# Zeroing and filling arrays of diagonals in DRAM, in large transfers or in parts, in a state-space scan kernel

## The chip, the cores and the metric

The kernel runs on one core of a Trainium2 chip. The metric is the device time of one execution in microseconds. The median of three runs before the change is 3376.29 us (3375.55 to 3376.74).

## The reference, cut to what matters

Two layers work on an image batch x of shape (4, 32, 32, 256). The second (linear attention, then a mixture of 16 experts) is not touched by the change. The first normalises x, multiplies it up to 512 channels, applies a 3 x 3 depthwise convolution and gelu, and runs a selective state-space scan over the 1024 positions of each image, with 64 states for each of the 512 channels:

```python
        proj = x @ w_x
        dt_raw, Bm, Cm = jnp.split(proj, [R, R + N], axis=-1)      # R = 16, N = 64
        dt = jax.nn.softplus(dt_raw @ w_dt + dt_bias)
        A = -jnp.exp(A_log)

        def step(h, inp):
            xt, dtt, Bt, Ct = inp
            dA = jnp.exp(dtt[:, :, None] * A)
            h = dA * h + (dtt * xt)[:, :, None] * Bt[:, None, :]
            y = jnp.einsum('bdn,bn->bd', h, Ct)
            return (h, y)
```

The change concerns Bt alone, and how it gets to one of the places where it is multiplied by dtt * xt.

## The kernel before

**Units, states and slots.** The scan is cut into 8 units: 4 images by 2 halves of 512 positions (`units`, L256; `u` or `w` is a unit's number, and odd units are second halves). In a unit, 64 states are gone through in turn, and in a state the 512 channels in four blocks of 128 (`m`). One state and one block is a slot; a unit has 64 x 4 = 256 slots, numbered `k` over everything and `at` within the unit.

**What a slot does.** ScalarE computes the decay, exp(dt A), for four slots ahead (`decay`, L925). The product dt x B of a state is made, for each of four groups of 128 positions (`j`), from `dtxT`, which lies with positions on the partitions: ScalarE scales it by B (`scale`, L903) into `bx`, and TensorE transposes it into a PSUM bank, three slots ahead (`turn`, L931). For the first group there are three ways, given for every state by a letter in `KINDS`: A is ScalarE; P is GpSimd (POOL, `scale_apart`, L913, tile `bxp`); D is TensorE alone, by multiplying `dtxT` with a diagonal matrix that carries B's 128 entries (L935). VectorE then runs the recurrence over 512 positions as one scan instruction (`scan`, L954). It writes into a ring of four states (`ring`, `RING = 4`). Behind a state's fourth block, GpSimd multiplies the state by C's row (L961), and in the first half of an image a small transfer saves the state's last column for the second half (L966, `last<-h`, 128 x 4 numbers). TensorE adds the states up by transposes that accumulate in PSUM, 11 slots behind (`add_up`, L968).

**The diagonals.** D needs, for each state n, a 128 x 128 matrix with B on its diagonal and zeros elsewhere. These matrices lie in DRAM, in two arrays of 64 matrices each, `diag_b[0]` and `diag_b[1]` (L247); unit w uses array w % 2. A tile of zeros is copied over each array once (`zero_diagonals`, L251: 4 MB each, rows of 512 B), at slots 4 and 14 (L1122). For every unit but the first, one transfer writes B's entries onto the 64 diagonals: 64 x 128 elements, 4 bytes each, with a step of 129 elements (L505, in `put_bc`). It follows the copy of B and C out of PSUM into the tile `bct` (L500) and the transfer of C into DRAM (L502, `cd<-bct`). `fetch_diagonal` (L897) loads a state's matrix, 64 KB, three states ahead, into one of three buffers.

**The SyncE queue.** All of these transfers are issued on SyncE's queue (SP), in program order, and an instruction that waits there holds all that follow. In a state SP issues C's row for three states on, spread over the partitions (`fetch`, L877, 256 KB, tile `cb_n`, four buffers), a diagonal matrix where the letter is D, and in first halves `last`; besides them loads of x, of the convolution's tap matrices (`dgc<-diags`, L402), of residual rows, and, in unit 6, the next layer's weights (L738 to L746).

**The order.** The order in each engine's stream is fixed when the program is built: the loop over slots (L1108) emits the slot's work, and then takes pieces of the other work (the next units' normalisation, convolution, projection and dt; the last unit's output) from lists made by `beside` (L995). A piece is (gap in slots from the one before, engine, cost, function, whether it takes or frees the spare PSUM bank, a thing it needs done). Each part of a list is spread evenly over a stretch of slots given in `EVEN`, `ODD` or `START`; of all lists whose next piece is due, the earliest is taken, within a budget for each engine and slot (`MOST`; SP's cost is 0). B and C of unit u + 1 are made in unit u by `dt_bc`'s first part (`dt0`); `dt1` begins at slot 50 in even units, 61 in odd ones and 52 in unit 0.

Of the kernel before, what the change touches and what calls it, by code (L numbers as in the profile page):

```python
# [16 lines left out]
P = 128  # L17
# [5 lines left out]
def over_middle(ap, n):  # L23

    return ap.unsqueeze(1).to_broadcast([ap.shape[0], n, ap.shape[1]])
# [8 lines left out]
def conv_ssm_attn_moe_kernel(ctx: ExitStack, tc: tile.TileContext, a: dict, out: bass.AP):  # L34
    nc = tc.nc
# [6 lines left out]
    NS = a["L0_conv_A_log"].shape[1]  # L42
# [4 lines left out]
    DK = DN // P  # L47
# [83 lines left out]
    def blk(i, n=BANK):  # L131
        return slice(i * n, (i + 1) * n)
# [12 lines left out]
    with ExitStack() as l0:  # L145
# [20 lines left out]
        with nc.allow_non_contiguous_dma(reason="small, once"):  # L166
            for m in range(DK):
                nc.scalar.dma_start(
                    out=cw[:, m, :],
                    in_=a["L0_conv_conv_w"][:, :, 0, m * P : (m + 1) * P].rearrange(  # L170
                        "i j p -> p (i j)"
                    ),
# [7 lines left out]
            out=w_dt[R : R + 1, :], in_=a["L0_conv_dt_bias"].rearrange("(o d) -> o d", o=1)  # L180
# [66 lines left out]
        diag_b = [dram.tile([NS, P, P], F32, name=f"diag_b{k}") for k in range(2)]  # L247
        zero = scanp.tile([P, P], F32, name="zero", tag="dgb", bufs=3)
        nc.vector.memset(zero, 0.0)

        def zero_diagonals(k):  # L251
            nc.sync.dma_start(
                out=diag_b[k].rearrange("n a b -> a n b"), in_=over_middle(zero, NS)
            )

        units = [(b, seg) for b in range(NB) for seg in range(NHALF)]  # L256
        made = {}
        done = set()
# [14 lines left out]
        def piece(gap, eng, cost, what, bank="", need=None):  # L273
            return gap, eng, cost, what, bank, need
# [6 lines left out]
        def logs(rs, mv):  # L281
            nc.scalar.activation(rs, mv, AF.Ln, bias=eps5)
# [172 lines left out]
        def dt_bc(w, needs):  # L455
# [42 lines left out]
            def put_bc():  # L498
                t = pre.tile([P, BANK], F32, name="bct")
                (nc.scalar.copy if on_scalar("bc") else nc.vector.tensor_copy)(t, made["bg"])  # L500
                cd = dram0.tile([NS, BANK], F32, name="cd")
                nc.sync.dma_start(out=cd, in_=t[NS:, :])  # L502
                if w > 0:
                    with nc.allow_non_contiguous_dma(reason="diagonals"):
                        nc.sync.dma_start(  # L505
                            out=diag_b[w % 2].rearrange("n a b -> n (a b)")[:, :: P + 1],
                            in_=t[:NS, :P],
                        )
                made["cd", w] = cd

            for j in range(TPB):
                for m in range(0, DK, 2):
# [117 lines left out]
            for m in range(DK):  # L630
# [3 lines left out]
                    lambda m=m: (put_dtx(m), done.add(("dt", w)) if m == DK - 1 else None), "free",  # L634
                ))
            return parts + [todo]

        def after_stats(u):
            made["mv"] = pre.tile([P, TPB, 2], F32, name="mv")
# [201 lines left out]
        def on_scalar(what):  # L841

            return not alone and what in APART[made["u"] % 2]
# [15 lines left out]
        at = [i for i, p in enumerate(conv_1) if p[4] == "free"][2] + 1  # L859
# [135 lines left out]
        def beside(u):  # L995


            n = len(units)
            v = u + 2
            made["u"] = u  # L1000
            at = START if u == 0 else ODD if u % 2 else EVEN
            dts = [at[f"dt{i}"] for i in range(5)]
            lists = [[([
                piece(1, "PE", 0.22, lambda m=m, j=j: skip(u, m, j))
                for m in range(DK) for j in range(TPB)
            ], at["skip"])]]
            if v < n:
                b, half = units[v]
                if u == 0:
                    lists.append([  # L1010
                        (head(b, 0), at["head"]), (head(b, 1), at["head1"]), (conv(v), at["conv"]),
                    ])
                elif half == 0:
                    lists.append([(head(b, 1), at["head"]), (conv(v), at["conv"])])
                else:
                    lists.append([(conv(v), at["conv"])])
                    if b + 1 < NB:
                        lists[-1].append((head(b + 1, 0), at["head"]))
            if v == n:
                lists.append([(matrices(), MATS)])  # L1020
            if u > 0:
                lists.append([(after_stats(u - 1), at["stats"])])
            if u + 1 < n:
                lists.append(list(zip(dt_bc(u + 1, ("st", u - 1) if u > 0 else None), dts)))
            else:
                lists.append([([
                    piece(1, "ACT", 1.5, lambda: logs(made["rs"], made["mv"][:, :, 1]),
                          need=("st", u - 1)),
                    piece(1, "ACT", 0.2, lambda: roots_after(u - 1)),
                ], dts[2])])  # L1030
            if u > 0:
                lists.append(list(zip(after(u - 1, ("rs", u - 1)), (at["after0"], at["after1"]))))
            return [
                [(lo + (hi - lo) * i / len(part), *p)
                 for part, (lo, hi) in l for i, p in enumerate(part)]
                for l in lists
            ]
# [55 lines left out]
        with tc.manual_schedule():  # L1093
            alone = False
            nc.scalar.preload_act_table_set("natural_log_exp_and_others")
            n_all = len(steps) * DK
            for s in range(4):
                fetch(s)
            for k in range(8):
                scale(*divmod(k, DK))  # L1100
            for s in range(4):
                scale_apart(s)
            for k in range(4):
                decay(*divmod(k, DK))
            for k in range(3):
                turn(*divmod(k, DK))
            lists, free, free_at, holds = [], True, 0, None
            for k in range(n_all + LAG):  # L1108
                u, at = divmod(k, SLOTS)
                if k + 8 < n_all:  # L1110
                    scale(*divmod(k + 8, DK))
                if k + 4 < n_all:
                    decay(*divmod(k + 4, DK))
                if k < n_all:
                    scan(*divmod(k, DK))
                    if k % DK == DK - 1 and k // DK + 4 < len(steps):
                        scale_apart(k // DK + 4)
                if k >= LAG:
                    add_up(*divmod(k - LAG, DK))
                if k + 3 < n_all:  # L1120
                    turn(*divmod(k + 3, DK))
                if k in (4, 14):  # L1122
                    zero_diagonals(1 if k == 4 else 0)
                if at % DK == 1 and k > DK and k // DK + 3 < len(steps):
                    fetch(k // DK + 3)
                    if by_diagonal(k // DK + 3, 0):
                        fetch_diagonal(k // DK + 3)
                if k >= LAG and at == LAG - 1 and u > 0:
                    close_sum(u - 1)
                if u == len(units):  # L1130
                    continue
                if at == FIRST:
                    lists = beside(u)
                    ready = [k] * len(lists)
                if at < FIRST:
                    continue
                used = dict.fromkeys(("PE", "DVE", "ACT", "POOL", "SP", ""), 0.0)
                while True:
                    best = None
                    for i, l in enumerate(lists):  # L1140
                        if not l or ready[i] + l[0][1] > k or l[0][0] > at and i != holds:
                            continue
                        when, _, eng, c, _, pb, need = l[0]
                        if need and need not in done:
                            continue
                        if pb == "take" and not (free and free_at < k):
                            continue
                        if used[eng] > 0 and used[eng] + c > MOST.get(eng, 9.0):
                            continue
                        if best is None or when < best[0]:  # L1150
                            best = when, i
                    if best is None:
                        break
                    i = best[1]
                    _, _, eng, c, what, pb, _ = lists[i].pop(0)
                    what()
                    ready[i] = k
                    used[eng] += c
                    if pb == "take":
                        free, holds = False, i  # L1160
                    elif pb == "free":
                        free, free_at, holds = True, k, None
                assert at < SLOTS - 1 or not any(lists), [len(l) for l in lists]
# [628 lines left out]
    for o in range(NB):  # L1792
        n = o + 1 if o + 1 < NB else None
# [407 lines left out]
    for e in (*range(SOON, NE), *range(SOON)):  # L2201
        todo += [k for k in fixed if k[1] == e]
        n = len({k[1] for k in todo if k not in soon})
# [46 lines left out]
```

## Time and profile before

| what | us |
|---|---|
| median of three runs | 3376.29 |
| profiled execution, its own time | 3389.96 |
| span of the profiled execution | 3387.8 |
| scan, first to last VectorE scan instruction (L954) | about 130 to 2690 |
| VectorE scans (L954), 2048 of 1.2 us and 1.26 us mean | 2387.7 busy |
| whole transfer of B's entries (L505), 7 of them, issue to landing | 15.9 median |
| `last<-h` (L966), 256 of them, issue to landing | 3.1 median |
| C's row (L880), 512 of them, issue to landing | 3.3 median |
| diagonal matrix (L900), 100 of them, issue to landing | 3.2 median |

The profile records one execution with start and end of every instruction. Busy time of an engine is the sum of its instructions; before each instruction the profile gives the engine's idle time and what ended it (the releaser). DMA transfers appear twice: as an instruction on the queue that issues them (SP), where a long duration means that the issue itself was held, and as a time from issue to landing. PE is the matrix engine and PEld its weight loads; DVE is VectorE, ACT is ScalarE, POOL is GpSimd. PEclk is the granted clock of TensorE, 1.00 being full.

### The profile page before, as it was taken

To read this page: it belongs to the slowest core of one execution; us is meant where nothing else is said; L and a number is where in the kernel's file an instruction comes from. 1 tells how busy PE (TensorE), PEld (TensorE's weight loads), DVE (VectorE), ACT (ScalarE), POOL (GpSimd) and SP (SyncE) were. 2 spreads that over 40 slices of the span, in tenths; PEclk is the share of its full clock that TensorE was granted. 3 is DMA by queue.
4 is the path that set the end of the run, shared out by engine and by line. 5 is a ranking of instruction groups with operands and counts; after the bars stand their busy time and mean duration, and the time that the engine had idled before them with its cause. 6 is when DMAs were issued, how large, how long until landed. Compare 5 with 4: busy or idle time off the path is not lost. (4 is left out here: it accounts for less than half of the span.)

```text
span 3387.8 us, 62750 instructions
## 1 busy us (share of the span) xinstructions
PE 3172.2 (94%) x23407; PEld 2753.3 (81%) x23407; DVE 2886.9 (85%) x3435; ACT 2717.3 (80%) x4621; POOL 2718.4 (80%) x1215
## 2 busy tenths in 40 slices
PE   7899999999999999999999999989999889789998
PEld 4588888988898888888988988768778756589998
DVE  4699999999999999999999999999999867652222
ACT  1699999999999999999999999899999754322221
POOL 0488998999999989999998999899999842234443
PEclk9999999999999999999999999999999999999999
DMA  3552224224333332253334223423222210467785
GB/s 105 150 68 63 68 66 69 71 71 62 67 78 69 68 72 76 62 63 74 73 73 68 71 64 60 71 54 68 60 62 67 80 48 29 156 186 231 214 245 149
DMA packets 423835, 300.76 MB, mean 89 GB/s; under 512 B 225073, under 2 KB 329393, under 8 KB 423522
## 3 DMA queue, kind: packets, MB, share of 16 engines
q1 hardware_dynamic: 397202, 274.25, 32.9%
q0 software_dynamic: 14016, 18.05, 2.8%
q10 hardware_dynamic: 12304, 4.37, 0.5%
q8 instruction: 187, 3.06, 0.4%
q14 instruction: 126, 1.03, 0.1%
HBM read 262.34 MB, written 34.87 MB: 88 GB/s over the span
## 5 line engine op out<-in xcount | busy, mean ns | idle before, releaser
L961 POOL TENSOR_TENSOR h<-h,cb_n 128x2048 f32<-128x2048 f32 x512 | 2154.9, 4226 | 142.6 <-DVE h L954 89.9
L928 ACT ACTIVATE da<-dt,l_conv_a_log_sb 128x512 f32<-128x512 f32 x2048 | 1438.3, 714 | 32.4 <-DVE h L954 31.3
L908 ACT ACTIVATE bx<-dtxT,proj 128x512 f32<-128x512 f32 x1748 | 1246.9, 714 | 29.9 <-DVE dtxT L600 16.4
L975 PE MATMUL y<-ident,h 128*128 128x128 f32 x8192 | 1236.5, 274 | 8.9 <-POOL h L961 5.8
L954 DVE TENSOR_TENSOR_SCAN h<-da,last,ps 128x512 f32<-128x512 f32 x1024 | 1217.9, 1262 | 7.0 <-PE ps L940 1.8
L954 DVE TENSOR_TENSOR_SCAN h<-da,ps 128x512 f32<-128x512 f32 x1024 | 1169.8, 1201 | 41.8 <-DMA last<-h 16.8
L940 PE MATMUL ps<-ident,bx 128*128 128x128 f32 x6992 | 1119.0, 276 | 41.7 <-DVE h L954 29.4
L975 PEld LDWEIGHTS y<-ident,h 128*128 128x128 f32 x8192 | 979.0, 141 | 99.9 <-issue 20.6
L940 PEld LDWEIGHTS ps<-ident,bx 128*128 128x128 f32 x6992 | 819.7, 142 | 101.8 <-DVE h L954 81.1
L2015 DVE TENSOR_TENSOR hT<-s,p 128x256 f32<-128x256 f32 x146 | 61.4, 421 | 281.0 <-ACT s L2014 281.0
L940 PE MATMUL ps<-ident,bxp 128*128 128x128 f32 x800 | 237.6, 297 | 58.9 <-DVE h L954 46.0
L2033 POOL DMA_INDIRECT out_dram<-yb,src x73 | 116.0, 1589 | 212.3 <-DVE yb L2030 82.2
L2014 ACT ACTIVATE s<-p 128x256 f32<-128x256 f32 x146 | 56.1, 384 | 265.4 <-PE p L2008 262.6
L413 PE MATMUL bg<-pad,dgc 128*128 128x256 f32 x864 | 258.2, 380 | 0.4 <-DMA dgc<-diags 0.4
L940 PEld LDWEIGHTS ps<-ident,bxp 128*128 128x128 f32 x800 | 112.3, 140 | 142.0 <-DVE h L954 89.2
L919 POOL TENSOR_SCALAR bxp<-dtxT,proj 128x512 f32<-128x512 f32 x200 | 147.0, 735 | 59.5 <-DVE dtxT L600 59.5
L935 PE MATMUL ps<-dgb,dtxT 128*128 128x128 f32 x800 | 170.3, 295 | 22.5 <-DMA dgb<-diag_b 9.7
L2008 PE MATMUL p<-xT,w 128*128 128x128 f32 x1408 | 171.7, 275 | 2.2 <-ACT xT L1988 2.2
L2008 PEld LDWEIGHTS p<-xT,w 128*128 128x128 f32 x1408 | 167.4, 192 | 5.0 <-ACT xT L1988 2.9
L935 PEld LDWEIGHTS ps<-dgb,dtxT 128*128 128x128 f32 x800 | 120.5, 190 | 49.2 <-DVE h L954 36.2
L413 PEld LDWEIGHTS bg<-pad,dgc 128*128 128x128 f32 x864 | 130.5, 191 | 0.7 <-DMA dgc<-diags 0.7
L2008 PE MATMUL p<-xT,m 128*128 128x128 f32 x928 | 115.4, 278 | 0.0
(341 smaller groups left out, 2681.6 us busy)
## 6 DMA issues: line engine op xcount, KB each, us to landing
cb_n<-cd SPq DMA_DIRECT2D x512, 256.0 KB, 3.3
m<-in_L_ffn_w_dram SPq DMA_DIRECT2D x87, 512.0 KB, 5.6
w<-in_L_ffn_w_dram SPq DMA_DIRECT2D x60, 512.0 KB, 6.9
dgc<-diags SPq DMA_DIRECT2D x84, 192.0 KB, 3.1
diag_b<-zero SPq DMA_DIRECT2D x2, 4096.0 KB
dgb<-diag_b SPq DMA_DIRECT2D x100, 64.0 KB, 3.2
last<-h SPq DMA_DIRECT2D x256, 2.0 KB, 3.1
xd<-xe SPq DMA_DIRECT2D x8, 512.0 KB, 3.5
```

The lines of the kernel that those rows point to most:

```text
L413: nc.tensor.matmul(made["bg"].rearrange("p (h w) -> p h w", w=WW)[:, blk(c, deep), :], made["dgc", m * 3 + i][:, j, :], pads[m][:, at : at ...
L908: nc.scalar.activation(t, made["dtxT", u][:, j, :], AF.Copy, scale=made["proj", u][:, j, R + n : R + n + 1])
L919: nc.gpsimd.tensor_scalar(t, made["dtxT", u][:, 0, :], made["proj", u][:, 0, R + n : R + n + 1], 1.0, ALU.mult, ALU.mult,)
L928: nc.scalar.activation(t, made["dt", u][:, m, :], AF.Exp, scale=A[:, m, n : n + 1])
L935: nc.tensor.matmul(t[:, blk(j, P)], made["dtxT", steps[s][0]][:, j, blk(m, P)], made["dgb", s], start=True, stop=True,)
L940: nc.tensor.transpose(t[:, blk(j, P)], made["bx", s, j][:, blk(m, P)], ident)
L954: nc.vector.tensor_tensor_scan(h[:, m, 1:], made.pop(("da", s, m)), made.pop(("dbx", s, m)), 0.0 if seg == 0 else last[b][:, n, m : m + 1] ...
L961: nc.gpsimd.tensor_tensor(h[:, :, :BANK], h[:, :, 1:], over_middle(made["c", s], DK), ALU.mult)
L975: nc.tensor.matmul(made["y", u][j][:, blk(m, P)], made["h", s][:, m, blk(j, P)], ident, is_transpose=True, start=n == 0 and m == 0, stop=n ...
L2008: nc.tensor.matmul(p12[:, j, s, :], w_of(w, key)[:, ck, blk(h + j, P)], on_b["xT", key][:, ck, :], start=(ck == 0), stop=(ck == CK - 1),)
L2015: nc.vector.tensor_tensor(on_b["hT", key][:, h : h + 2, :], s, p12[:, :, 1, :], ALU.mult)
L2033: s = nc.gpsimd.indirect_dma_start(of[:, :], bass.IndirectOffsetOnAxis(src[:, c : c + 1], 0), yb, None, bounds_check=NB * L - 1, oob_is_er ...
```

## The change

The 4 MB transfers of zeros are cut into eight parts each, of 8 states (1024 rows of 512 B). They are issued at the third slot of each of the first 16 states, array 1 first. The transfer of B's entries is cut into eight parts too, of 8 states x 128 elements. They are taken out of `put_bc` and become pieces of a list of their own on SP, at least 4 slots apart, spread over 40 slots from the first slot of `dt1` on; they need the copy into `bct`. Transfers that write and read the arrays keep their content.

```diff
-        def zero_diagonals(k):
+        part_of = NS // 8
+
+        def zero_part(i):
+            k, n = 1 - i // 8, (i % 8) * part_of
             nc.sync.dma_start(
-                out=diag_b[k].rearrange("n a b -> a n b"), in_=over_middle(zero, NS)
+                out=diag_b[k][n : n + part_of].rearrange("n a b -> a n b"),
+                in_=over_middle(zero, part_of),
             )
...
                 cd = dram0.tile([NS, BANK], F32, name="cd")
                 nc.sync.dma_start(out=cd, in_=t[NS:, :])
-                if w > 0:
-                    with nc.allow_non_contiguous_dma(reason="diagonals"):
-                        nc.sync.dma_start(
-                            out=diag_b[w % 2].rearrange("n a b -> n (a b)")[:, :: P + 1],
-                            in_=t[:NS, :P],
-                        )
+                made["bct", w] = t
                 made["cd", w] = cd
+                done.add(("bct", w))
...
+        def entries(w):
+
+            def part(i):
+                with nc.allow_non_contiguous_dma(reason="diagonals"):
+                    nc.sync.dma_start(
+                        out=diag_b[w % 2].rearrange("n a b -> n (a b)")[
+                            blk(i, part_of), :: P + 1
+                        ],
+                        in_=made["bct", w][blk(i, part_of), :P],
+                    )
+
+            return [piece(4, "SP", 0, lambda i=i: part(i), need=("bct", w)) for i in range(8)]
...
                 lists.append(list(zip(dt_bc(u + 1, ("st", u - 1) if u > 0 else None), dts)))
+                lists.append([(entries(u + 1), (at["dt1"][0], at["dt1"][0] + 40))])
...
-                if k in (4, 14):
-                    zero_diagonals(1 if k == 4 else 0)
+                if k % DK == 2 and k // DK < 16:
+                    zero_part(k // DK)
```

## The prediction

> **What bounds the kernel now.** I read, in order: busy time by stretches, who waited for whom at the scan line, SyncE's instructions around the two kinds of transfer that the change cuts up, and VectorE's instructions at the same moments.
>
> The stretches first (columns: stretch, its length, then busy us of PE, PEld, DVE, ACT, POOL with counts, granted TensorE clock, DMA share, GB/s).
>
> ```profile
> 1000.00:1300.00 300.00, 292.18 (x2304) 264.22 (x2303) 296.60 (x272) 290.81 (x467) 282.96 (x102) 1.00 0.33 71
> 1300.00:1600.00 300.00, 285.06 (x2255) 256.89 (x2254) 294.14 (x276) 292.69 (x475) 289.13 (x112) 0.99 0.35 68
> ```
>
> From about 130 to 2690 us VectorE works 98 to 99% of the time. It is the bound of the state scan, with the others a few per cent behind; the span follows what keeps VectorE idle. SyncE (SP) only issues transfers, so its work costs nothing until something on VectorE's path waits for it. What the scan's VectorE instructions waited for (us, times):
>
> ```profile
>   DMA last<-h: 16.8, 5
>   PE ps L940: 10.3, 40
>   ACT da L928: 8.9, 18
> ```
>
> The largest item is five waits for the small transfer that saves a state's last column (L966). It reads the slot of the ring of four that VectorE wants to overwrite four states later. SyncE at those moments (start, us on SP, queue, line, operation):
>
> ```profile
> 135.25 0.62 SPq L252 DMA_DIRECT2D diag_b<-zero  x1
> 138.80 10.24 SPq L880 DMA_DIRECT2D cb_n<-cd  x1
> ...
> 152.99 0.69 SPq L252 DMA_DIRECT2D diag_b<-zero  x1
> 153.78 14.46 SPq L966 DMA_DIRECT2D last<-h  x1
> ...
> 195.38 0.60 SPq L505 DMA_DIRECT2D diag_b<-bct  x1
> 196.07 9.96 SPq L966 DMA_DIRECT2D last<-h  x1
> ```
>
> Ordinarily an L966 issue takes 0.6 us and an L880 issue 0.32. Straight behind a transfer of 8192 rows (zeros: 128 x 64 rows of 512 B; B's entries: 64 x 128 elements of 4 B) the next issue is held for 10 to 14 us, and SP issues in order. VectorE then (in brackets its idle time before, and the releaser):
>
> ```profile
> 170.82 4.55 DVE L954 TENSOR_TENSOR_SCAN h<-da,ps 128x512 f32<-128x512 f32 x4 [5.83 <-DMA last<-h]
> 211.57 3.44 DVE L954 TENSOR_TENSOR_SCAN h<-da,ps 128x512 f32<-128x512 f32 x3 [2.81 <-DMA last<-h]
> 846.16 4.55 DVE L954 TENSOR_TENSOR_SCAN h<-da,ps 128x512 f32<-128x512 f32 x4 [2.35 <-DMA last<-h]
> 2126.25 5.67 DVE L954 TENSOR_TENSOR_SCAN h<-da,ps 128x512 f32<-128x512 f32 x5 [3.01 <-DMA last<-h]
> 2134.37 0.69 DVE L552 TENSOR_SCALAR dt<-bg 128x512 f32<-128x512 f32 x1 [2.46 <-PE bg L541]
> ```
>
> The fifth wait is at 1487.00, 2.82 us. So of seven transfers of entries only those in units 0, 2, 4 and 6 stall VectorE; units 1, 3 and 5 are second halves of a batch and save no column. There the held instruction is a load of C's row (L880), and only POOL waits, 0.92 to 1.51 us, which VectorE doesn't feel.
>
> **What goes: the zeros.** The two transfers of 4 MB become 16 of 512 KB (1024 rows each). The 5.83 us go, and 0.52 us just after. Before it, ScalarE sat 4.78 us for a load of x stuck in the same queue; VectorE felt 0.87 + 0.28 us of that. Together 7.5 us. Not all can return: from 142 to 168 us PE is nearly without a gap (projections and skip products besides the scan's own), and VectorE already lost 2.02 us to it at 154. At 165, where the stall starts, PE was three slots ahead, which gives VectorE 3.4 us at 1.14 a scan before it meets PE again. I take 6.0, with 4 and 7.5 as ends.
>
> **What goes: the entries.** Waits at units 0, 2, 4, 6: 2.81 + 2.35 + 2.82 + 3.01 = 11.0 us. VectorE has no larger gap in the tens of us behind the first three, so nothing takes the time back there. Unit 6 has a tail: 2.46 + 0.33 + 1.01 = 3.8 us of waits for PE, because PE, idle for 2.86 us behind the stall, came back slow (same columns as the stretches above):
>
> ```profile
> 2126.00:2132.00 6.00, 4.47 (x18) 3.50 (x19) 5.67 (x5) 4.50 (x8) 3.61 (x2) 0.65 0.98 264
> 2132.00:2138.00 6.00, 6.00 (x25) 5.02 (x24) 3.60 (x4) 2.46 (x4) 3.10 (x1) 0.50 0.90 199
> ```
>
> [...] The row shows clock 0.65, then 0.50, and three transposes at 0.85 us instead of 0.49; the row decides, so the tail goes with the stall. Sum 11.0 + 3.8 = 14.8 us. [...]
>
> **What is added on SP.** 16 + 56 issues instead of 9, at some 0.6 us each: 63 x 0.6 = 38 us of SP over all, none of it on VectorE's path. The entries start 195.38 and 829.67 us lie 512 slots apart, 1.24 us a slot; so parts of entries come every 5 slots = 6.2 us, parts of zeros every 4 = 5.0 us. SP's own work in a state is about 0.95 us (0.32 + 0.6); it has room. Behind a part wait, in order on SP, the next column save (L966), C row (L880), tap matrices (L402) or diagonal (L900).
>
> How long is the next issue held? From the whole (0.6 + 10 us until the next issue is through) by count: 10.6 / 8 = 1.3 us. The nearest row of the right size is the loading of the conv's weights at the start (L168, 128 x 9 = 1152 elements of 4 B): four issues on ScalarE's queue took 7.19 us in all, 1.8 us each, and landed after 5.7 us. I take 1.8 and 5.7. Below, the column save itself (512 elements of 4 B) is issued in 0.6 and lands in 3.1.
>
> [...]
>
> [...] The margin of a column save is read at the stalls: issued (started) at 196.07 and wanted at 211.57 - 2.81 = 208.76, 12.7 us; likewise 13.4, 13.1 and 11.6 in units 2, 4, 6, and 11.2 at the zeros. [...] C rows have about as much: held 8 to 10 us, they made POOL wait at most 1.5. [...]
>
> The diagonals have no such cover: PE waited for them 12 times, 9.7 us in all, up to 1.6. [...] I take 1.3 us, ends 0 and 9. An entries part also waits for its array's zeros and for the copy of B: the last zeros of array 1 are issued at slot 30, the first entries at 52, and no part is placed ahead of the copy, which is done by 195 us in unit 0, where the whole transfer goes out behind some 50 slots; so neither wait costs anything. The other engines' instructions and their order are untouched, since a piece on SP takes no bank and no budget.
>
> **Sum.** 6.0 + 14.8 - 1.3 = 19.5 us out of the profiled execution's 3389.96 us (span 3387.8): 3370.5. That execution is 13.7 us above the median of the runs, 3376.29; the stalls belong to queue and ring, not to the profiler, so I take the same 19.5 off the median: 3356.8.
>
> **Rivals.** (a) The forecast: 3357, its own range 3350 (7.5 + 14.8 + 3 of smaller waits) to 3363 (4 + 11 - 2). Chance 0.70. (b) The stalls vanish but VectorE meets the next engine: ScalarE and PE are at 95 to 98% in the same stretches, and half is given back. For it: the pile of 0.2 us waits for PE and ScalarE at 930 to 1050. Against: none follow the four stalls directly. 20.8 / 2 = 10.4 less 1.3: 3367. Chance 0.13. (c) It doesn't do what it says: the small transfers at the stall points queue as before, or the diagonals eat the 9 us and the tail stays: 4 + 11 - 9 to 0, so 3370 to 3376, say 3374. Chance 0.10. (d) Slower: a part holds SP not by its count but as long as the whole does. Then SP needs 10.6 + 1.2 us for each 6.2 us, 5.6 behind after each part, 45 after eight; less the 8 us spare, 37 a unit, 7 x 37 = 259 us: 3636. It decides from a hold of about 5 us (6.2 less 1.2). Against it: 1.8 us for 1152 elements. Chance 0.07, nearly all of it nearer to the threshold than to 3636.
>
> **Numbers.** A measurement of this kernel can tell about 0.2%, 6.8 us, from no change: faster means below 3369.5. Faster: 0.70 + 0.10 of (b) = 0.80; same: (c) and the rest of (b), 0.13; slower 0.07. The range 3350 to 3373 leaves out (d), most of (c)'s upper half, and 0.04 below.
>
> **What would show it.** [...] I am wrong if column saves still arrive late at any part, if waits for diagonals grow past 20 us, or if VectorE's idle time moves to PE or ScalarE instead of leaving.

## The result, and the profile after

Medians of eight runs each: 3375.64 us before, 3365.97 us after; ratio 0.9971, 95% interval 0.9961 to 0.9981. The change makes the kernel 9.7 us (0.29%) faster. The forecast was 3357, a gain of 19.3 us. The stated range, 3350 to 3373, holds the time; the forecast's own range, 3350 to 3363, does not, and the gain is half of what the sum said.

The profile of after tells another story than the medians. Its execution took 3366.33 us, within 0.4 us of the median; the profiled execution before took 3389.96, 13.7 above the median of the three runs shown with it. Between the two profiles lie 23.6 us, more than forecast.

What the scan's VectorE instructions waited for, after (us, times; the scan is L967 there):

```profile
  PE ps L953: 8.6, 41
  ACT da L941: 7.7, 17
  ACT bx L921: 1.5, 7
  POOL bxp L932: 0.2, 1
  DMA last<-h: 0.2, 1
```

The 16.8 us behind the column save have become 0.2; apart from another 0.2 behind POOL no item is larger than it was. SP in the busiest stretch, where parts of zeros (L255) and of entries (L642) overlap in unit 0:

```profile
199.07 0.33 SPq L893 DMA_DIRECT2D cb_n<-cd  x1
199.45 0.33 SPq L642 DMA_DIRECT2D diag_b<-bct  x1
199.83 1.97 SPq L255 DMA_DIRECT2D diag_b<-zero  x1
201.90 0.60 SPq L979 DMA_DIRECT2D last<-h  x1
203.38 0.34 SPq L893 DMA_DIRECT2D cb_n<-cd  x1
203.77 0.44 SPq L255 DMA_DIRECT2D diag_b<-zero  x1
204.27 0.48 SPq L642 DMA_DIRECT2D diag_b<-bct  x1
204.84 3.22 SPq L979 DMA_DIRECT2D last<-h  x1
```

Of 256 column saves the longest issue is now 3.22 us instead of 14.46. And unit 6, where the clock had fallen to 0.65 and 0.50 (stretch, length, busy us of PE, PEld, DVE, ACT, POOL, granted clock, DMA share, GB/s; the parts of entries come from 2105 on):

```profile
2096.00:2102.00 6.00, 5.92 (x49) 4.94 (x47) 6.00 (x7) 6.00 (x11) 6.00 (x3) 1.00 0.91 263
2102.00:2108.00 6.00, 5.97 (x48) 4.98 (x47) 6.00 (x7) 5.53 (x10) 6.00 (x3) 1.00 0.65 134
...
2104.00:2150.00 46.00, 43.70 (x318) 34.97 (x317) 45.85 (x48) 42.95 (x69) 40.67 (x16) 1.00 0.34 54
```

VectorE has next to no idle time in it and the clock is full. The last scan instruction starts at 2664.5 us instead of 2690.6. So in the profiles the stalls that the prediction listed are gone; the question is why the median moved by only half of that.

### The profile page after: what moved, and what is told of

Read it like the earlier page. It is cut to its first block, busy times and chain, and to the rows that moved or that the text cites. A ratio compares the mean times of both kernels' runs of the same rounds, so it can differ in the third digit from the quotient of the medians.

```text
span 3364.4 us, 62834 instructions
## 1 busy us (share of the span) xinstructions
PE 3169.8 (94%) x23407; PEld 2751.8 (82%) x23407; DVE 2885.4 (86%) x3435; ACT 2714.8 (81%) x4621; POOL 2718.1 (81%) x1215
## 5 line engine op out<-in xcount | busy, mean ns | idle before, releaser
L967 DVE TENSOR_TENSOR_SCAN h<-da,last,ps 128x512 f32<-128x512 f32 x1024 | 1217.7, 1257 | 6.9 <-PE ps L953 1.5
L967 DVE TENSOR_TENSOR_SCAN h<-da,ps 128x512 f32<-128x512 f32 x1024 | 1169.1, 1200 | 20.9 <-PE ps L953 7.1
```

What stands on the lines that cost most here:

```text
L967: nc.vector.tensor_tensor_scan(h[:, m, 1:], made.pop(("da", s, m)), made.pop(("dbx", s, m)), 0.0 if seg == 0 else last[b][:, n, m : m + 1] ...
```

## The experiments

They were made in four sessions, each with its own runs of the kernel before beside it; a ratio is always against those.

**First session: two causes apart.** Four kernels. The first is the kernel before, unaltered, profiled anew.

> The kernel before, unchanged, profiled afresh. The change took 9.7 us off the median but 23.4 us off the profiled span, and the profiled execution before stood 13.7 us above its median while the one after stands at its median. Theory T (trace inflated): the stalls in the old trace are longer than in ordinary executions; this fresh profile again lies 10 to 15 us above its own timed runs and again shows about 17 us of waits for the column save. Rival G (given back): the trace is typical, the stalls are as long in every run and half of the gain is given back in ordinary runs by something the profile of after hides; then this profile shows the 17 us and its time lies within 3 us of the timed runs. Rival O (odd execution): the first profile was one slow execution; the fresh one lies near 3376 with waits for the column save well under 17 us. Ratio to before 1.000 in all.

Measured: 3388.88 us, beside runs of the kernel before at 3389.55 (3384.92 to 3398.20); ratio 1.0004 (0.9996 to 1.0012). None of the three theories holds as put. The kernel before took 13 us longer in the first session, in all of the 36 runs beside it, and its profile shows the stalls of the first profile: 14.3 us of waits for the column save, holds of 9 to 14 us. So the first profile seems to come from such a session, and the three times shown with it from another; it is not one of those three runs.

That it was an odd execution of a quick session, one in which the kernel before takes some 3376 us, is the less likely reading. Such sessions do have slow executions (3389.05 and 3392.28 us among the 38 of the second), but with a mean granted clock of 0.984. At the first profile's 0.988 the 29 executions of the kernel before in the other three sessions took at most 3383.7 us, the 7 in this one 3384.2 to 3391.2.

The second has the zeros in parts and the entries as before:

```diff
+                if w > 0:
+                    with nc.allow_non_contiguous_dma(reason="diagonals"):
+                        nc.sync.dma_start(
+                            out=diag_b[w % 2].rearrange("n a b -> n (a b)")[:, :: P + 1],
+                            in_=t[:NS, :P],
+                        )
                 made["bct", w] = t
...
-                lists.append([(entries(u + 1), (at["dt1"][0], at["dt1"][0] + 40))])
```

> The zeros in 16 parts, the entries whole in their old place. By my sum the zeros are worth 6.0 of 20.8 us and the entries 14.8. If ordinary runs keep that proportion at half size (T), about 3 us of the 9.7 come here: ratio 0.9991. If the entries' stalls hardly exist outside the profiler, nearly all of the 9.7 come here: 0.9972. If the sum holds in full and half is given back (G): 6 us here, 0.9982. In the profile the four waits of units 0, 2, 4 and 6 stay, the 5.83 us one goes.

Measured: 3383.32 us, ratio 0.9980 (0.9973 to 0.9987): 6.2 us by the medians. The term of the forecast was 6.0.

The third has the entries in parts and the zeros as before:

```diff
...
-                if k % DK == 2 and k // DK < 16:
-                    zero_part(k // DK)
+                if k in (4, 14):
+                    zero_diagonals(1 if k == 4 else 0)
```

> The zeros whole as before, the entries in 56 parts. By my sum 14.8 - 1.3 = 13.5 us: ratio 0.9960. At half size (T) 6.7 us: 0.9980. If only the zeros' stall is real in ordinary runs: 1.000. In the profile only the 5.83 us wait behind the zeros stays, and the clock of unit 6 stays at 1.00.

Measured: 3378.57 us, ratio 0.9974 (0.9962 to 0.9987): 11.0 us by the medians, 8.8 by the ratio. The forecast was 13.5.

The fourth is the change without any entries:

```diff
-                lists.append([(entries(u + 1), (at["dt1"][0], at["dt1"][0] + 40))])
```

> Leaves out writing B's entries onto the diagonals altogether (the matrices stay zero, so the D states lack their first 128 positions' input); the zeros in parts. What the 56 parts still cost: if they are free (my forecast: 1.3 us, ends 0 and 9) the time is that of after, 3366, down to 3364.7; if the missing half of the gain is lost to the parts (rival G by contention on SP or DMA), 3356 to 3358, ratio 0.994 to 0.995.

Measured: 3366.36 us, ratio 0.9936 (0.9923 to 0.9949), 23.2 us below the kernel before beside it (21.7 by the ratio), and the same time as after has elsewhere. From the first to the last scan instruction its profile takes 2535.7 us, that of after 2534.7: the 56 parts cost nothing that can be seen. That the time without stalls is the same in this slow session suggests that the session's 13 us lie in the stalls; the third session tests it.

The gains of the two halves, 6.2 and 11.0 us, add up to 17.2, six less than the 23.2. The executions of these two kernels spread over 12.6 and 15.5 us, and no run shows where the six lie.

**Second session: what about the cut matters.** Here the kernel before took 3377.44 us.

> The changed kernel itself, unaltered, beside the kernel before on one chip. The kernel before has now been timed at 3375.6 in the runs of the verdict and at 3389.6 beside the first four experiments, which are not profiled runs alone: so the 13.7 us are not the profiler's. Theory S (setting): the length of the holds differs between the chips or sessions on which the runs were made; the changed kernel has no holds, takes about 3366 to 3370 wherever it runs, and gains 18 to 22 us where the kernel before takes 3389 (ratio 0.994) and about 10 where it takes 3376 (0.997). Rival U (uniform): everything is slower by 13 us where the kernel before is; then after takes about 3380 there, ratio 0.997 again.

Measured: 3366.27 us, ratio 0.9969 (0.9958 to 0.9979), 11.2 us: the first result once more.

The next kernel issues a unit's eight parts one straight behind the other:

```diff
-            return [piece(4, "SP", 0, lambda i=i: part(i), need=("bct", w)) for i in range(8)]
+            return [piece(
+                4, "SP", 0, lambda: [part(i) for i in range(8)], need=("bct", w)
+            )]
```

> The change, but a unit's eight entries parts are issued one straight behind the other at the first of the 40 slots, not 5 slots apart. If cutting is what matters (each part is short, others get in between on the DMA engines), it takes as long as after. If spreading is what matters, as my forecast has it (rows on the queue in a short time are what holds SP), SP is held about as long as by the whole, VectorE waits 2 to 4 us in each of units 0, 2, 4 and 6, and the time is that of the zeros-in-parts kernel: 8 to 14 us above after. [...]

Measured: 3380.97 us, ratio 1.0013 (1.0004 to 1.0022): 14.7 us above after and even above the kernel before. SP of this kernel in unit 0, and VectorE's waits:

```profile
193.21 13.40 SPq L642 DMA_DIRECT2D diag_b<-bct  x8
206.70 1.44 SPq L895 DMA_DIRECT2D cb_n<-cd  x1
```
```profile
  DMA last<-h: 10.7, 5
```

Eight issues one behind the other take SP 12.1 to 13.8 us in units 0, 2, 4 and 6; the whole, with the hold behind it, took 10.2 to 12.4 in the first profile. Spreading is what removed the hold; cutting alone made it longer.

The next one has four parts of 16 states:

```diff
-                        out=diag_b[w % 2].rearrange("n a b -> n (a b)")[
-                            blk(i, part_of), :: P + 1
-                        ],
-                        in_=made["bct", w][blk(i, part_of), :P],
+                        out=diag_b[w % 2].rearrange("n a b -> n (a b)")[blk(i, 16), :: P + 1],
+                        in_=made["bct", w][blk(i, 16), :P],
...
-            return [piece(4, "SP", 0, lambda i=i: part(i), need=("bct", w)) for i in range(8)]
+            return [piece(4, "SP", 0, lambda i=i: part(i), need=("bct", w)) for i in range(4)]
```

> The change with four entries parts of 16 states instead of eight of 8, at 10 slots' distance. [...] If both use 16 engines, a part of 16 holds twice as long, 2.6 to 3.6 us, still within the 8 us spare: the same time, but L979's longest issue is about twice as long in the profile.

Measured: 3365.86 us, ratio 0.9970 (0.9959 to 0.9981); the same as after. A part of 16 lands after 4.8 us (median of 28). The landing of parts of 8 was recorded in no profile; the longest column save, 3.80 us, is near after's 3.22 and not twice as long. How many DMA engines a part uses is not shown.

The last one issues the whole transfer on ScalarE's queue (the cut is against the kernel with only the zeros in parts):

```diff
                     with nc.allow_non_contiguous_dma(reason="diagonals"):
-                        nc.sync.dma_start(
+                        nc.scalar.dma_start(
                             out=diag_b[w % 2].rearrange("n a b -> n (a b)")[:, :: P + 1],
                             in_=t[:NS, :P],
```

> Zeros in parts; a unit's entries whole, in their old place, but issued on ScalarE's queue instead of SP's. [...] If the hold is of the DMA engines that all queues share, column saves land late all the same and the time is that of the zeros-in-parts kernel, 8 to 14 us above after.

Measured: 3366.75 us, ratio 0.9972 (0.9964 to 0.9979), the same as after, with a wider spread of its runs (3363.62 to 3375.89). By time alone that says little, since in a quick session the whole on SP costs only 3.8 us more than after (fourth session, below). The profile says more. The whole takes 16.1 us to land, as long as in the first profile (15.9), but SP's longest column save is this one:

```profile
192.82 4.26 SPq L985 DMA_DIRECT2D last<-h  x1
```

Behind the whole on SP it took 9.6 to 11.8 us in the first profile, and VectorE now waits 0.7 us in all for column saves. So most of the hold was felt only on the queue on which the many rows were issued.

**Third session: the stalls where the kernel before is quick.**

> The kernel before, profiled once more, beside the changed one on one chip. Theory S (setting): the time of the kernel before goes with the length of its holds on SP. If it is timed near 3376 here, its profile shows holds shorter than the 10 to 14 us of the first profile and VectorE's waits for the column save near half of 16.8 us or less; if it is timed near 3389, they are as in the first profile. Rival: the holds are the same in both and the 13 us lie elsewhere, for instance in the second layer behind 2690 us, which would then be longer by that much.

Measured: 3377.17 us, ratio 0.9998 (0.9989 to 1.0007), beside 3377.30. This is a profile of the kernel before in a quick session. The landing of its whole transfers of entries:

```profile
DMA to landing us min/median/max: 13.6/14.0/14.4
```

That of the first profile's:

```profile
DMA to landing us min/median/max: 15.9/15.9/16.3
```

The holds behind them in units 0, 2, 4 and 6 are 9.20, 8.04, 9.00 and 8.87 us, against 9.96, 10.82, 11.76 and 9.59 in the first profile. Unit 0's:

```profile
197.00 9.20 SPq L966 DMA_DIRECT2D last<-h  x1
```

VectorE in this profile:

```profile
154.62 3.44 DVE L954 TENSOR_TENSOR_SCAN h<-da,ps 128x512 f32<-128x512 f32 x3 [1.69 <-DMA last<-h]
161.26 2.33 DVE L954 TENSOR_TENSOR_SCAN h<-da,ps 128x512 f32<-128x512 f32 x2 [3.20 <-ACT da L928]
172.36 7.89 DVE L954 TENSOR_TENSOR_SCAN h<-da,ps 128x512 f32<-128x512 f32 x7 [4.12 <-ACT bx L908]
...
210.16 3.44 DVE L954 TENSOR_TENSOR_SCAN h<-da,ps 128x512 f32<-128x512 f32 x3 [0.48 <-DMA last<-h]
...
2118.08 5.67 DVE L954 TENSOR_TENSOR_SCAN h<-da,ps 128x512 f32<-128x512 f32 x5 [2.18 <-DMA last<-h]
```

Behind the entries of units 2 and 4 there is no wait any more, behind unit 0's 0.48 us, behind unit 6's 2.18 us. PE was idle for 2.03 us there, its clock stayed at 1.00, and there is no tail. Sum 2.7 us where the first profile had 14.8. The zeros, in contrast, cost as much as ever: 1.69 + 3.20 + 0.53 + 0.23 + 4.12 = 9.8 us from 152 to 173 us. Together 12.4 us.

The rival, that the sessions differ somewhere else, fails too. From the first to the last scan instruction the kernel before took 2560.6 us in the first profile, 2560.2 in the first session's and 2547.8 here. What lies outside the scan is not shorter here: 834.6 us, against 827.2 and 828.4.

> The changed kernel on the same chip. By S it takes 3364 to 3370 here too, wherever the kernel before stands: ratio 0.994 beside 3389, 0.997 beside 3376. By U (all is slower by the same) the ratio is 0.997 in both.

Measured: 3366.21 us, ratio 0.9965 (0.9953 to 0.9977), 11.1 us by the medians. Between first and last scan instruction these two profiles differ by (2678.4 - 130.6) - (2663.4 - 128.2) = 12.6 us, which is the sum of the stalls. The whole profiled executions differ by more (3384.48 and 3363.64); the other 8 us lie ahead of the scan and behind it, where the change does nothing, and the medians don't show them.

**Fourth session: the proportion.** It was on the same chip as the first session, where the kernel before had taken 3389.55; now it took 3377.24.

> Zeros in parts, entries whole, now wanted beside a kernel before of either time. In the fresh profile of a kernel before with median 3377 the whole transfer of entries landed in 14.0 us instead of 15.9 and VectorE waited behind it 0.5 and 2.2 us in units 0 and 6 and not at all in 2 and 4, while the stall behind the zeros was as long as ever, some 8 to 9.5 us. So beside 3376 to 3378 nearly all of the gain is the zeros': 7 to 9 of about 10.5 us, ratio 0.9974 to 0.9980. Beside 3389 it is 6 to 7, as first measured. If instead the proportion of my forecast holds everywhere (6.0 of 20.8), it is 3 us beside 3377, 0.9991.

Measured: 3368.74 us, ratio 0.9971 (0.9961 to 0.9982), 8.5 us by the medians. Its whole entries landed in 13.2 us. The first session ran the same kernel on the same chip. VectorE's waits for the column save were then 9.8 us (at the end of the line) and are now 2.3:

```profile
L973 DVE TENSOR_TENSOR_SCAN h<-da,ps 128x512 f32<-128x512 f32 x1024 | 1169.2, 1201 | 32.4 <-DMA last<-h 9.8
```
```profile
  DMA last<-h: 2.3, 1
```

The holds behind the whole were 10.0 to 10.8 us then and are 8.1 to 8.4 now. So the hold behind the entries varies with the session, in one kernel on one chip. That it is all of the 14.6 us between this kernel's two medians is not shown: the execution profiled in the first session was its quickest, 3378.01 us.

> The changed kernel on the same chip as the one above. Beside 3376 to 3378: 3366 again, so what is left to the entries is 1 to 4 us. Beside 3389: the case not measured yet for this kernel; by theory S 3366 to 3370, ratio 0.994, the forecast's 19.5 us; by U 3380, 0.997.

Measured: 3364.94 us, ratio 0.9960 (0.9946 to 0.9974), 12.3 us. What is left to the entries here is 3.8 us, against 11.0 in the first session.

All in one table (medians, us below the kernel before of the same session):

| session | before | zeros in parts | entries in parts | both, the change |
|---|---|---|---|---|
| first (same chip as fourth) | 3389.6 | 6.2 | 11.0 | not run; 23.2 with no entries at all |
| second | 3377.4 | | | 11.2 |
| third | 3377.3 | | | 11.1 |
| fourth | 3377.2 | 8.5 | (3.8, the remainder) | 12.3 |

The changed kernel was never timed beside a kernel before at 3389, so that it gains some 20 us there is an inference from the kernel without entries and from the first pair of profiles; the parts' own gains add up to 17.2.

## Why the prediction was right, and where it was half wrong

**What bounds the kernel: right.** VectorE's idle time set the end. Taking the waits away moved the last scan by what the waits had been, in both pairs of profiles: 25.9 us between first and last scan instruction in the first pair, where the waits of the first profile add up to 16.8 + 0.52 + 0.87 + 0.28 + 3.8 + 2.02 = 24.3 (the 2.02 I had put down to PE); 12.6 in the third session's, where the list has 12.4.

**The failing step: the entries' term, carried from the profiled execution to the median.** I wrote "the stalls belong to queue and ring, not to the profiler, so I take the same 19.5 off the median". The first half is right: nothing in the runs points to the profiler. The second does not follow. The profiled execution stood 13.7 us above the median of the three runs, and I took this gap for a constant. As far as the profiles show, it was stall: the scan of the first profile is 12.8 us longer than that of the third session's. Without the stalls the changed kernel takes 3365 to 3366 us in four sets of runs. In the kind of session that I was asked about the entries' term measures 2.7 us (third session's profile), not 14.8. With the zeros' 8.5 that makes 11.2, where 9.7 to 12.3 was measured. A gap of 0.4% between the profiled execution and the runs was two thirds of the expected gain; I should have asked which of my terms could hold it.

**Where the range was lucky.** The measured time lies above the forecast's own range, whose end was 3363. It lies inside the whole range only because that was widened to 3373 for rivals (b) and (c), and neither of their mechanisms came true. The nearest point, (b)'s 3367, is a coincidence.

**Why the entries' term varies so much: a threshold.** VectorE waits only for what a hold goes beyond the slack of its column save. Hold less wait gives that slack: 7.2, 8.5, 8.9 and 6.6 us in units 0, 2, 4 and 6 of the first profile. I had put it at 8 or more (the 8 us spare in (d): the shortest margin, 11.2 us, less 3.1 for the landing); behind these holds the save took 4.2 to 5.5 us from the end of its issue to VectorE's start. Holds of 10.0, 10.8, 11.8 and 9.6 us left waits of 2.8, 2.4, 2.8 and 3.0; the third session's, 0.7 to 2.8 us shorter, left 0.5, 0, 0 and 2.2. In unit 0 the hold is only 0.8 us shorter; there the save itself also landed sooner, 4.0 us behind its issue instead of 5.5. I had the margins from issue to want in the text and used them for the parts, where there was room, but not for the whole, where 2.4 to 3.0 us of excess were everything. What makes the holds of a session longer or shorter is not known; the same chip showed both, 10.0 to 10.8 us in the first session and 8.1 to 8.4 in the fourth.

**The zeros' term: the stall right, its size too low.** I took 6.0 with ends 4 and 7.5, because PE seemed loaded and 2.02 us at 154 were put down to PE. In the changed kernel VectorE runs through that stretch with one gap of 0.24 us, so these 2.02 us were the zeros' too (two later profiles of the kernel before name the column save for them). The profiles give 9.5 and 9.8 us, the medians 6.2 and 8.5.

**The clock's tail: right that it goes with the stall, but no fixed cost.** A gap of 2.86 us on PE was followed by a clock of 0.65 and 0.50 in the first profile, one of 3.33 by this in the first session:

```profile
2126.16 0.48 PE L940 MATMUL ps<-ident,bxp 128*128 128x128 f32 x1 [3.33 <-DVE h L954]
```
```profile
2125.00:2131.00 6.00, 4.84 (x19) 3.86 (x20) 5.55 (x5) 4.86 (x8) 2.99 (x2) 0.50 0.97 283
```

One of 2.03 us, in the third session, was followed by a full clock:

```profile
2119.36 0.33 PE L940 MATMUL ps<-ident,bxp 128*128 128x128 f32 x1 [2.03 <-DVE h L954]
```
```profile
2118.00:2124.00 6.00, 4.53 (x29) 3.33 (x30) 5.92 (x6) 4.92 (x9) 4.50 (x2) 1.00 1.03 307
```

The length of the one gap did not decide: with only the entries in parts a gap of 1.77 us at 158 us (one of 0.73 lay 3.5 us before it) was followed by 0.50, while in the first profile one of 1.91 us at 213 was followed by 1.00. A lowered clock need not cost much either. Behind unit 6 of the first session's kernel with zeros in parts it fell to 0.75 and 0.68 after a gap of 3.21 us, and VectorE waited 0.76 us for PE, not 3.8.

**The price of the parts: right, 0 instead of 1.3.** No run shows the 1.3 us that I took off, nor its upper end of 9: PE's waits for diagonals were 9.7 us before and 9.9 after. The kernel without entries takes 3366.36 us, the changed one 3365 to 3366. SP's issues of parts take 0.33 us in the median, not 0.6. The longest column save takes 3.2 us, in unit 0, where parts of zeros are in flight as well; in units 2, 4 and 6 a save behind a part takes at most 2.0, near the 1.8 that I took.

**The rivals.** Half came back, yet not by (b)'s mechanism: no other engine took the time, the waits for PE and ScalarE did not grow. Nor by (d): parts issued back to back do hold SP, but eight of them for 12.1 to 13.8 us, not for eight times the whole's hold. And not by (c): no column save queued as before, and PE's waits for diagonals stayed at 9.9 us.

## What to carry to other kernels

Many small rows on a queue held what was issued straight behind them there, 8.0 to 15.6 us behind 8192 rows in these runs; spread them over the time between two uses, or put them on a queue that nothing urgent uses, and don't only cut them. A wait that exceeds its slack by little is not a fixed number: write down hold, landing and slack apart, and expect every microsecond of hold to count once the slack is used up (units 4 and 6 here: 2.8 and 0.7 us less hold, 2.8 and 0.8 us less wait). And when the profiled execution stands off the runs by as much as the gain that is forecast, the gap itself has to be explained by the terms of the sum before any of them is carried over.

## What the runs showed of the hardware that was not expected

The time of a transfer of 8192 elements of 4 bytes into DRAM is not constant: medians of 13.2, 14.0 and 15.9 us from issue to landing in three profiles, for the same shape on SP's queue. The same chip gave 3389.6 us and, in a later session, 3377.2 for one unaltered kernel. On ScalarE's queue the transfer took as long to land (16.1 us), but SP's longest column save took 4.3 us instead of some 10.
